# A timetable of slots repacked: latents, routing and the first half of the expert blocks moved to other slots

## The chip, the cores and the metric

The kernel runs on one core of a Trainium2 chip, in float32. Its time is the device time of one execution in microseconds (us). Three executions of the kernel before were timed; one more was taken with the hardware profiler, and all rows shown here come from that one.

The engines are named as the profile names them: PE is TensorE (PEld its weight loads), DVE is VectorE, ACT is ScalarE, POOL is GpSimd, SP is SyncE, which issues most DMAs. Each engine works through its own list of instructions in order. When an instruction waits for a semaphore, everything behind it on the same engine waits too.

## What is computed

Two decoder layers on x of 32 sequences of 128 tokens, width 128. Layer 0: self attention, cross attention over a context, gated experts. Layer 1: causal attention, then an attention of latents over context and latents (2 heads of 64), then 8 ReLU experts of which each token uses two. Only the last two parts matter here, and in outline they are:

```python
# L1 latents: x is both residual and latents; per sequence
ln  = layernorm(layernorm(x))
q, k_l, v_l = split(ln @ [Wq, Wlkv])         # 128 queries, 128 latent keys
k, v = concat(context_kv, (k_l, v_l))        # 256 keys
attn = softmax(mask(rmsnorm(q) @ rmsnorm(k).T))
x = x + (attn @ v) @ Wo + bo
# L1 experts
probs = softmax(layernorm(x) @ router_w + router_b)
topk_w, topk_i = top_k(probs, 2); topk_w /= topk_w.sum()
h = relu(xf @ w1[e] + b1[e]); y = h @ w2[e] + b2[e]
x = x + sum over the token's two experts of gate * y
```

## The kernel before

**Groups and slots.** The 32 sequences ("batches") form 8 groups of 4 (`NG = 4`, `G = 8`). The three attention stages run as one software pipeline over 192 numbered slots, two per batch. Everything else is written into a dictionary `plan` by `at(slot, phase, fn)` and is issued while the loop passes that slot. The phases of a slot come in the order open, pre, (the slot's own score products), inner, (the weighted sums), mid, post. There is no scheduler that reorders: the slot and the phase fix the place in every engine's list. A slot has no fixed length; it lasts as long as the slowest engine needs for what stands in it. After slot 197 no attention is left and a slot holds only what was planned there.

**Stage ends.** `done(2, g)` is the slot after which group g's causal attention is in `X[g]`: 145, 153, ... 201 for groups 0 to 7.

**Latents (`latent_attention`).** Group g starts at `d = done(2, g) + LATER`, with `LATER = 2`. The statistics, normalisation, transposes and the product with `w_lat` take slots d to d + 5. `square`, `total` and `root` give the squared norms of the heads (ACT, DVE, then a power on POOL, L1089); `unit_heads` divides by them at d + 6 or d + 7, phase mid. Then each of the four batches takes four slots, started every second slot from d + 8: `turn` (transposes of q and k, L1136), `score` (L1145, L1150, maxima L1156, exponentials L1157), `turn_e` (L1164, L1166), `weigh` (L1176, L1181). Each of these takes PSUM banks from the pool `ps_m`, which has three. `fetch` loads the batch's context keys and values (`lkv`, 3 buffers) from DRAM two slots ahead of `turn`. `leave` and `project` (L1111, L1118) write the group's result into X at d + 18 and d + 19.

**Routing (`router`).** Groups are routed in units, `UNITS = [(0, 1), (2, 3), (4, 5), (6,), (7,)]`. After the last group of a unit has been projected, the steps `stats`, `scale`, `apply`, `turned`, `choice`, `choose2`, `choose3`, `ranks` follow about one per slot. `ranks` yields for each token and each of its two experts a row of a DRAM array `slots0` (groups 0 to 3) or `slots1` (groups 4 to 7). `scatter` then writes 128 rows with one indirect DMA issued on POOL (L1679), 8 per group, two per slot. A running count per expert, `carry`, passes from unit to unit. `gates_over` and `bias` (L1692, L1705) add the experts' output bias to X.

**Expert blocks (`experts`, `expert_blocks`).** Each half of the tokens is worked off in `NB = 23` blocks of 256 rows. `table` computes from the counts which expert and which rows each block has. `fetch_w` (514 KB, tile `w`, 4 buffers) and `fetch_x` (130 KB, tile `bx`, 10 buffers) are issued on SP, each after a register load from the table. A block takes one slot: `turn(j + 1)` in pre (L1826), `hidden(j)` in inner (L1836, with bias and ReLU shared by ACT and DVE, L1844 and L1846), `result(j - 1)` in post (L1853; scaled by the gates into tile `bo`, 4 buffers, L1861 on ACT and L1863 on DVE), and `leave(j - 2)` in mid: two indirect DMAs on POOL (L1868) that write the rows back to token order. The weights of block j + 3 and the rows of block j + 5 are fetched in post. At slot 203 `swap` closes the pool of the attention tiles and opens the pool `blocks` in the same memory.

```python
            at(done(2, G - 1) + 2, "open", swap)
            begins = [done(2, G // 2 - 1) + 40, done(2, G - 1) + 33]
```

So the first half begins at slot 209 (its first `hidden` stands in slot 211), the second at 234 (first `hidden` in 236). The scatters of the first half's last unit stand in slots 200 to 207, those of the second half's last group in 230 to 233. `gather`, `finish` and `store` add the rows of both experts to X and write the output; for the first half's groups they stand among the second half's blocks, for the second half's they follow the last block.

Of the kernel before, what the change touches and what calls it, by code (L numbers as in the profile page):

```python
# [11 lines left out]
F32 = mybir.dt.float32  # L12
# [10 lines left out]
P = 128  # L23
B, S, D = 32, 128, 128
DC = 96
NG = 4
G = B // NG
# [81 lines left out]
def decoder(ctx: ExitStack, tc: tile.TileContext, a: dict, out: bass.AP):  # L109
# [898 lines left out]
    def latent_attention(lazy, kv, row, bias, masked, plan_route):  # L1008

        LATER = 2  # L1010
        V = []

        def opened():
            if not V:
                for r in range(2):
                    v = lazy["lat"].tile([P, NG, HL, DL + 1], F32, tag=f"v{r}", name=f"lv{r}", bufs=1)
                    nc.gpsimd.memset(v, 1.0)
                    V.append(v)
            return lazy["lat"]

        def plan_group(at, g, d):
            m = {}

# [55 lines left out]
            def flat(u):  # L1079
                return m["qk"][:, 2 * u : 2 * u + 2].rearrange("p b s d -> p (b s d)")  # L1080
# [19 lines left out]
            for u in range(2):  # L1100
                at(d + 4 + u, "mid", square(u))
                at(d + 5 + u, "mid", lambda u=u: m["total", u]())
                at(d + 5 + u, "mid", root(u))
                at(d + 6 + u, "mid", lambda u=u: unit_heads(flat(u), n4, m["nrm", u]))
            for i in range(NG):
                plan_batch(at, m, g, i, d + 8 + 2 * i)

# [13 lines left out]

            at(d + 18, "mid", leave)
            at(d + 19, "mid", project)
            plan_route(at, g, d + 19)

        def plan_batch(at, m, g, i, t):
            b, s = g * NG + i, {}

            def fetch():
                s["kv"] = opened().tile([P, KV], F32, tag="kv", name="lkv", bufs=3)  # L1130
                nc.sync.dma_start(s["kv"][:, P:], kv[b : b + 1].rearrange("b p w -> p (b w)"))
# [36 lines left out]
            def weigh():  # L1168
                if i == 0:
                    m["on"] = opened().tile([P, NG, D], F32, tag="on", name="lon", bufs=1)  # L1170
                vc = s["kv"][:, 2 * P :].rearrange("p (h w) -> p h w", h=HL)
                av = bank(ps_m)[:, : HL * (DL + 1)].rearrange("p (h w) -> p h w", h=HL)
                for h in range(HL):
                    for c in range(2):
                        v = m["v"][:, i, h, :] if c == 0 else vc[:, h, :]
                        nc.tensor.matmul(  # L1176
                            av[:, h, :], s["eT"][:, 2 * h + c, :], v,
                            start=(h == 0 and c == 0), stop=(c == 1), skip_group_check=True,
                        )
                rz = small.tile([P, HL], F32, tag="lrz", name="lrz")  # L1180
                nc.vector.reciprocal(rz, av[:, :, DL])  # L1181
                nc.vector.tensor_tensor(
                    m["on"][:, i, :].rearrange("p (h d) -> p h d", d=DL), av[:, :, :DL], wide(rz, [P, HL, DL], 2), ALU.mult
                )
# [7 lines left out]
        def beside(at, done):  # L1192
            for g in range(G):
                plan_group(at, g, done(2, g) + LATER)
        return beside
# [329 lines left out]
    N2 = 2 * NG  # L1525
    UNITS = [(0, 1), (2, 3), (4, 5), (6,), (7,)]
    HALVES = [(0, 1), (2, 3, 4)]

    def router(slots, lazy):
# [8 lines left out]
        def plan_route(at, g, t):  # L1538
# [198 lines left out]
            def turned(u):  # L1737
# [3 lines left out]
                return fn  # L1741

            for u in us:
                at(t + 1 - 8 * (us[-1] - u), "mid", stats(u, 0))
                at(t + 2 - 8 * (us[-1] - u), "pre", stats(u, 2))
            at(t + 2, "mid", scale)
            for u in us:
                at(t + 3 + u, "mid", apply(u, 0))
                at(t + 4 + u, "pre", apply(u, 2))
                at(t + 4 + u, "mid", turned(u))  # L1750
            t += us[-1]
            at(t + 5, "mid", choice)
            at(t + 6, "mid", choose2)
            if len(groups) > 1:
                t += 1
            at(t + 6, "mid", choose3)
            at(t + 7, "mid", ranks)
            n = 0
            for k in range(n2):
                for c in range(2):  # L1760
                    at(t + 8 + n // 2, ("pre", "inner")[n % 2], scatter(c, k))
                    n += 1
            for u in us:
                at(t + 8 + u, "mid", gates_over(u))
                at(t + 9 + u, "mid", bias(u))

        return plan_route, [carry[units[-1]] for units in HALVES]

    def expert_blocks(f, total, lazy):
# [5 lines left out]
        def table():  # L1775

            def row(shape, tag, dtype=F32):
                return lazy["blocks"].tile([1] + shape, dtype, tag="tb_" + tag, name="tb_" + tag, bufs=2 if tag == "where" else 1)

# [68 lines left out]
        def result(j):  # L1848
            s = state[j]
            ps = bank(ps_t)  # L1850
            for u in range(2):
                for c in range(4):
# [3 lines left out]
                    )  # L1856
            o = s["o"] = lazy["blocks"].tile([P, 2, D], F32, tag="o", name="bo", bufs=4)
            for u in range(2):
# [31 lines left out]
    def experts(halves, lazy, heads, late):  # L1890

        def beside(at, done):
# [3 lines left out]

            at(done(2, G - 1) + 2, "open", swap)
            begins = [done(2, G // 2 - 1) + 40, done(2, G - 1) + 33]

            def plan_half(f):  # L1900
# [3 lines left out]
                for j in range(3):  # L1904
                    at(t - 3 + j, "post", lambda j=j: fetch_w(j))
                for j in range(5):
# [217 lines left out]
```

## Time and profile before

| what | value |
|---|---|
| timed executions | 1186.5, 1189.68, 1194.54 us; median 1189.68 |
| the profiled execution's own time | 1213.03 us |
| its span, first to last instruction | 1211.2 us |
| mean granted TensorE clock | 0.951 |
| PE busy | 1107.3 us, 91% of the span |
| DVE busy | 808.4 us, 67% |
| POOL busy | 632.4 us, 52% |
| ACT busy | 572.9 us, 47% |
| last score product of the attention (L584) starts | 885.2 us |
| first block's `hidden` (L1836) starts | 949.95 us |
| second half's first `hidden` starts | 1097.25 us |
| last product of the blocks (L1853 group) ends | 1185.5 us |

How to read it: the profiled execution lies 23.4 us above the median of the timed ones, so a row of the profile is not by itself a piece of the time that is measured. A busy PE is not a PE at full speed: the column PEclk of the stretches gives the share of the clock that was granted in each. The clock came in two values here, 1.0 and 0.5.

### The profile page before, as it was taken

The numbers are of one execution on the slowest core, as the hardware profiler recorded it, in microseconds if no ns is written. First come the engines' busy times: TensorE is split into PE (matmuls) and PEld (weight loads), VectorE is DVE, ScalarE is ACT, GpSimd is POOL, SyncE is SP. The second block draws the span as 40 slices with busy tenths as digits, with TensorE's granted clock in tenths as the row PEclk, the third lists the DMA queues.
The fourth block names the chain that finished last, engine by engine and source line by source line (L and its number), as shares of the span: only waits on it lengthen the run. The fifth ranks groups of instructions, "written<-read, shape, count | busy, mean of one in ns | idle before, by whom it ended". The sixth has DMA issues, their size and how long they took to land. (4 is left out here: it accounts for less than half of the span.)

```text
span 1211.2 us, 30676 instructions
## 1 busy us (share of the span) xinstructions
PE 1107.3 (91%) x11923; PEld 818.1 (68%) x11923; DVE 808.4 (67%) x2290; ACT 572.9 (47%) x1302; POOL 632.4 (52%) x905
## 2 busy tenths in 40 slices
PE   8999999999999999999999999989988898888991
PEld 3576776676666676656666666666666688777991
DVE  4688888777877877677667678768666564353441
ACT  2355556666655555554445655644553432322330
POOL 3654555344345335434637664746747356664663
PEclk8899999999999999999999999989987898898996
DMA  7705333101021100111020000000102244445873
GB/s 201 240 22 178 99 99 99 54 28 37 3 45 45 46 21 18 37 37 37 2 50 2 11 15 14 15 10 28 32 19 98 93 141 129 145 142 161 256 227 107
DMA packets 83081, 92.09 MB, mean 76 GB/s; under 512 B 14274, under 2 KB 70264, under 8 KB 82928
## 3 DMA queue, kind: packets, MB, share of 16 engines
q1 hardware_dynamic: 77936, 81.57, 23.1%
q0 software_dynamic: 4992, 8.48, 2.0%
q8 instruction: 96, 1.57, 0.5%
q14 instruction: 57, 0.47, 0.1%
HBM read 53.84 MB, written 38.01 MB: 76 GB/s over the span
## 5 line engine op out<-in xcount | busy, mean ns | idle before, releaser
L595 ACT ACTIVATE e<-bank 128x512 f32<-128x512 f32 x384 | 208.1, 595 | 221.6 <-PE bank L584 213.6
L587 DVE TENSOR_REDUCE msc<-bank 128x4 f32<-128x512 f32 x384 | 245.8, 681 | 68.5 <-PE bank L584 67.0
L584 PE MATMUL bank<-kb,qz 32*128 32x256 f32 x1536 | 237.5, 412 | 7.8 <-DVE msc L587 6.1
L584 PE MATMUL bank<-qa,kb 32*128 32x128 f32 x3072 | 233.4, 288 | 1.6 <-ACT e L595 1.6
L584 PEld LDWEIGHTS bank<-qa,kb 32*128 32x128 f32 x3072 | 194.7, 190 | 4.5 <-ACT e L595 3.5
L584 PEld LDWEIGHTS bank<-kb,qz 32*128 32x128 f32 x1536 | 141.9, 189 | 78.8 <-issue 42.2
L1868 POOL DMA_INDIRECT y<-bo,bx x92 | 91.7, 997 | 87.7 <-ACT bo L1861 65.8
L612 PE MATMUL bank<-e,vt 128*32 128x128 f32 x3072 | 126.5, 282 | 2.4 <-POOL e L598 2.4
L598 POOL TENSOR_SCALAR_AFFINE_SELECT e<-e 128x512 f32<-128x512 f32 x128 | 79.1, 642 | 94.4 <-ACT e L595 94.2
L1853 PE MATMUL bank<-w,bh 128*128 128x128 f32 x736 | 95.4, 285 | 1.0 <-issue 0.9
L1853 PEld LDWEIGHTS bank<-w,bh 128*128 128x128 f32 x736 | 92.7, 201 | 4.8 <-issue 3.3
L1836 PE MATMUL bank<-bxT,w 128*128 128x256 f32 x368 | 93.0, 396 | 2.7 <-DVE bh L1846 1.0
L612 PEld LDWEIGHTS bank<-e,vt 128*32 128x32 f32 x3072 | 73.0, 110 | 27.8 <-POOL e L598 3.9
L1679 POOL DMA_INDIRECT slots<-rows,r_ati x64 | 63.8, 997 | 32.6 <-issue 16.5
L1836 PEld LDWEIGHTS bank<-bxT,w 128*128 128x128 f32 x368 | 69.9, 201 | 13.2 <-issue 2.0
L891 POOL TENSOR_TENSOR h<-h,g 128x512 f32<-128x512 f32 x30 | 37.6, 1271 | 71.5 <-DVE nm_st L798 44.8
L1846 DVE TENSOR_SCALAR bh<-bank,w 128x256 f32<-128x256 f32 x92 | 40.2, 478 | 43.9 <-PE bank L1836 35.1
L1861 ACT ACTIVATE bo<-bank,bx 128x128 f32<-128x128 f32 x46 | 16.9, 367 | 96.8 <-PE bank L1853 56.5
L323 ACT ACTIVATE xn<-x,ln_nb,ln_rs 128x128 f32<-128x128 f32 x96 | 42.1, 494 | 41.0 <-POOL ln_nb L317 41.0
L493 DVE SCALAR_TENSOR_TENSOR qa<-bank,head_rows,qz 128x128 f32<-128x128 f32 x192 | 57.6, 342 | 2.2 <-PE bank L485 2.2
L1844 ACT ACTIVATE bh<-bank,w 128x256 f32<-128x256 f32 x92 | 38.6, 471 | 40.1 <-PE bank L1836 15.1
L1157 ACT ACTIVATE le<-bank,lmx 128x256 f32<-128x256 f32 x64 | 26.9, 471 | 64.1 <-DVE lmx L1156 56.7
(322 smaller groups left out, 2280.9 us busy)
## 6 DMA issues: line engine op xcount, KB each, us to landing
w<-in_w_f SPq DMA_DIRECT2D x46, 514.0 KB
slots<-nowhere SPq DMA_DIRECT2D x8, 2340.0 KB
g<-spread SPq DMA_DIRECT2D x16, 512.0 KB
bx<-slots SPq DMA_DIRECT2D x46, 130.0 KB
kv<-kcv SPq DMA_DIRECT2D x8, 516.0 KB
lkv<-kv SPq DMA_DIRECT2D x32, 129.0 KB
y<-y SPq DMA_DIRECT2D x16, 256.0 KB
x<-in_x SPq DMA_DIRECT2D x8, 256.0 KB
```

Source lines behind the costliest of these rows:

```text
L323: nc.scalar.activation(m["xn"][:, i, :], X[g][:, i, :], AF.Identity, scale=m["rs"][:, i : i + 1], bias=m["nb"][:, i : i + 1])
L493: nc.vector.scalar_tensor_tensor(s["qa"][:, u, :], s["mp"][:, :P], head_rows[:, 1 - u : 2 - u], m["qz"][:, u, i * P : (i + 1) * P], ALU.mu ...
L584: nc.tensor.matmul(o, l, r, start=start, stop=stop, skip_group_check=True)
L587: nc.vector.tensor_reduce(tops(MSC[bb % 4], 2 * h + j), sc[j].rearrange("p (s n k) -> p s n k", s=2, n=2), AX.X, ALU.max, negate=True)
L595: nc.scalar.activation(e.rearrange("p n q -> p (n q)"), tr[j], AF.Exp, scale=SCALE)
L598: nc.gpsimd.affine_select(out=e, in_=e, compare_op=ALU.is_ge, fill=0.0, base=0, pattern=[[0, 4], [1, P]], channel_multiplier=-1)
L612: nc.tensor.matmul(s3["av"][32 * n : 32 * n + 32, h3 * P : (h3 + 1) * P], m3["vt"][:, i3, h3, n, u, :], es[u][:, n, :], start=(h3 == 0 and ...
L1679: ins = nc.gpsimd.indirect_dma_start(slots[f], bass.IndirectOffsetOnAxis(ap=m["ati"][:, c, n : n + 1], axis=0), m["rows"][c][:, n, :], Non ...
L1836: nc.tensor.matmul(ps[:, c * BLOCK : (c + 1) * BLOCK], s["w"][:, (2 * k + c) * P : (2 * k + c + 1) * P], s["xT"], start=True, stop=True,)
L1846: nc.vector.tensor_scalar(s["h"][:, n, :], p, bias, 0.0, ALU.add, ALU.max)
L1853: nc.tensor.matmul(ps[:, u * P : (u + 1) * P], s["h"][:, c, u * P : (u + 1) * P], s["w"][:, 512 + c * P : 512 + (c + 1) * P], start=(c == ...
L1868: ins = nc.gpsimd.indirect_dma_start(y, bass.IndirectOffsetOnAxis(ap=s["x"][:, u, D : D + 1].bitcast(U32), axis=0), s["o"][:, u, :], None, ...
```

## The change

In slots, before and after:

| | before | after |
|---|---|---|
| latents of group g start | done + 2 | done + 2, group 7: done |
| first batch's `turn` | d + 8 | d + 6 |
| batches per slot | one every second slot | group 7: one per slot |
| `unit_heads` | mid | pre of the same slot |
| units of routing | (4, 5) together | (4,) and (5,) |
| steps of routing | about one per slot | two per slot, in mid and the next pre |
| scatters of unit (2, 3) | 200 to 207 | 195 to 202 |
| scatters of group 7 | 230 to 233 | 220 to 223 |
| swap of the pools | 203 | 202 |
| first half: table, weights, rows, first `hidden` | 205, 206 to 208, 209, 211 | 199, all three at 202, 203, 205 |
| second half: the same | 230, 231 to 233, 234, 236 | 222, 223 to 225, 226, 228 |
| last `hidden` of the first half | 233 | 227 |

The buffers of `lkv` go from 3 to 6, of the latents' `lon` from 1 to 2, of `bo` from 4 to 6. The small tiles of `table` move to the pool `route`, since the table is now made before the pool `blocks` exists. Gather, finish and store of the first half keep their distance from the second half's begin.

```diff
@@ latent_attention
+        steps = [2] * (G - 1) + [1]
...
-            m = {}
+            m, step = {}, steps[g]
...
-                at(d + 6 + u, "mid", lambda u=u: unit_heads(flat(u), n4, m["nrm", u]))
+                at(d + 6 + u, "pre", lambda u=u: unit_heads(flat(u), n4, m["nrm", u]))
             for i in range(NG):
-                plan_batch(at, m, g, i, d + 8 + 2 * i)
+                plan_batch(at, m, g, i, d + 6 + step * i)
...
-            at(d + 18, "mid", leave)
-            at(d + 19, "mid", project)
-            plan_route(at, g, d + 19)
+            end = d + 6 + step * (NG - 1) + 4
+            at(end, "mid", leave)
+            at(end + 1, "mid", project)
+            plan_route(at, g, end + 1)
...
-                s["kv"] = opened().tile([P, KV], F32, tag="kv", name="lkv", bufs=3)
+                s["kv"] = opened().tile([P, KV], F32, tag="kv", name="lkv", bufs=6)
...
-                    m["on"] = opened().tile([P, NG, D], F32, tag="on", name="lon", bufs=1)
+                    m["on"] = opened().tile([P, NG, D], F32, tag="on", name="lon", bufs=2)
...
-                plan_group(at, g, done(2, g) + LATER)
+                plan_group(at, g, done(2, g) + (LATER if steps[g] > 1 else 0))
@@ router
-    UNITS = [(0, 1), (2, 3), (4, 5), (6,), (7,)]
-    HALVES = [(0, 1), (2, 3, 4)]
+    UNITS = [(0, 1), (2, 3), (4,), (5,), (6,), (7,)]
+    HALVES = [(0, 1), (2, 3, 4, 5)]
...
+            steps = []
             for u in us:
-                at(t + 1 - 8 * (us[-1] - u), "mid", stats(u, 0))
-                at(t + 2 - 8 * (us[-1] - u), "pre", stats(u, 2))
-            at(t + 2, "mid", scale)
+                ago = 8 * (us[-1] - u)
+                at(t - ago, "post", stats(u, 0))
+                at(t + 1 - ago, "pre", stats(u, 2))
+            steps.append(scale)
             for u in us:
-                at(t + 3 + u, "mid", apply(u, 0))
-                at(t + 4 + u, "pre", apply(u, 2))
-                at(t + 4 + u, "mid", turned(u))
-            t += us[-1]
-            at(t + 5, "mid", choice)
-            at(t + 6, "mid", choose2)
-            if len(groups) > 1:
-                t += 1
-            at(t + 6, "mid", choose3)
-            at(t + 7, "mid", ranks)
+                steps += [apply(u, 0), apply(u, 2)]
+            steps += [turned(u) for u in us]
+            steps += [choice, choose2, choose3, ranks]
+            for n, fn in enumerate(steps):
+                at(t + 1 + (n + 1) // 2, ("mid", "pre")[n % 2], fn)
+            t += 1 + (len(steps) + 1) // 2
...
-                    at(t + 8 + n // 2, ("pre", "inner")[n % 2], scatter(c, k))
+                    at(t + n // 2, ("pre", "inner")[n % 2], scatter(c, k))
...
-                at(t + 8 + u, "mid", gates_over(u))
-                at(t + 9 + u, "mid", bias(u))
+                at(t + u, "mid", gates_over(u))
+                at(t + 1 + u, "mid", bias(u))
@@ expert_blocks
-                return lazy["blocks"].tile([1] + shape, dtype, tag="tb_" + tag, name="tb_" + tag, bufs=2 if tag == "where" else 1)
+                return lazy["route"].tile([1] + shape, dtype, tag="tb_" + tag, name="tb_" + tag, bufs=2 if tag == "where" else 1)
...
-            o = s["o"] = lazy["blocks"].tile([P, 2, D], F32, tag="o", name="bo", bufs=4)
+            o = s["o"] = lazy["blocks"].tile([P, 2, D], F32, tag="o", name="bo", bufs=6)
@@ experts
-            at(done(2, G - 1) + 2, "open", swap)
-            begins = [done(2, G // 2 - 1) + 40, done(2, G - 1) + 33]
+            at(done(2, G - 1) + 1, "open", swap)
+            begins = [done(2, G - 1) + 2, done(2, G - 1) + 2 + NB]
...
-                    at(t - 3 + j, "post", lambda j=j: fetch_w(j))
+                    at(t - 3 + j if f else t - 1, "post", lambda j=j: fetch_w(j))
```

## The prediction

> **What bounds the kernel now.** I read the page first. PE is busy 91% of the span, so the question is which of its time is not work. The changed slots lie behind the last score product (885.2 us) and before the last block, so I asked for stretches of that part:
>
> ```profile
> core 0: us, PE busy (x) PEld busy (x) DVE busy (x) ACT busy (x) POOL busy (x), PEclk, DMA share, GB/s
> 918.00:950.00 32.00, 24.55 (x115) 16.78 (x114) 20.59 (x68) 14.67 (x39) 24.52 (x33) 0.72 0.41 130
> 950.00:1012.00 62.00, 60.11 (x420) 53.96 (x420) 33.11 (x109) 21.39 (x55) 26.89 (x33) 0.95 0.36 117
> 1012.00:1042.00 30.00, 24.63 (x124) 21.49 (x124) 13.02 (x54) 5.18 (x13) 19.86 (x24) 0.77 0.37 120
> 1042.00:1075.00 33.00, 31.95 (x221) 28.56 (x220) 18.87 (x74) 11.02 (x28) 21.03 (x26) 1.00 0.52 170
> 1075.00:1104.00 29.00, 20.10 (x108) 16.58 (x108) 6.88 (x18) 5.56 (x14) 14.61 (x15) 0.82 0.42 128
> 1104.00:1184.00 80.00, 80.00 (x563) 75.67 (x562) 35.51 (x89) 25.57 (x64) 47.83 (x46) 1.00 0.70 219
> ```
>
> The last row is the yardstick: blocks alone, PE full, clock 1.00, a block every 3.73 us (`hidden` at 1105.65 and 1109.39). Three rows fall short of it, in busy time and in clock: 918 to 950 (latents alone, before the first block), 1012 to 1042 (inside the first half), 1075 to 1104 (between the halves).
>
> To size the loss I price PE's list at the spacing of starts that the same lines show at full clock: 0.111 us for a float32 pass of 128 columns, 0.216 for 256, 0.324 for 384. So priced, PE's list holds 39.2 us of work from the last score product to the first `hidden`, 113.8 from there to the second half's first, 79.8 after it. The trace took 64.7, 147.3 and 88.3. Lost: **25.5, 33.5 and 8.5 us**.
>
> The timelines of PE, ACT and SP, and the waits of 885 to 1104, tell what the second loss is:
>
> ```profile
> 1016.40 0.31 PE L1653 MATMUL bank<-r_both,ones 128*128 128x32 f32 x2 [1.07 <-issue]
> 1018.02 0.37 ACT L1861 ACTIVATE bo<-bank,bx 128x128 f32<-128x128 f32 x1 [8.33 <-remote]
> ```
> ```profile
> ACT bo L1861 <- remote: 22.5, 4, 8.3
> ```
> ```profile
> 1086.27 3.73 PE L1853 MATMUL bank<-w,bh 128*128 128x128 f32 x32
> 1095.26 0.66 PE L1826 MATMUL bank<-ident,bx 128*128 128x128 f32 x2 [5.25 <-DMA bx<-slots]
> ```
>
> Four times ACT stands still, 22.5 us in all, for a releaser the profile can't name, while PE waits between two products that depend on nothing new ("issue") and SP takes 0.7 us for a register step that elsewhere takes 0.03. The profiled execution is 23.4 us above the median: I take these stops as belonging to it, not to a timed run. Without them 67.5 - 22.5 = **45 us are lost**, 25.5 of them before the first block.
>
> **The change, part by part.**
>
> *Work moved.* The changed PE list, priced the same way, holds 27.8, 116.5 and 81.7 us: 226.0 against 232.8, so 6.8 us (a batch's latents and routing of groups 2 to 4) now stand among the last score products. PE is nearly full there, so I count them as moved, not saved. Before the first `hidden` stand 11.4 us less: group 7's `w_lat` product 2.6, some three batches' steps 7.4, and others. They now stand beside blocks.
>
> *The first hole.* Before, PE reached 27.8 us of this work at about 926 us, 13 us lost; the other 11.4 us took it until 950, 12.5 lost. Those 12.5 are what the earlier blocks can fill. At one place a rule stands against so much: the Trainium skill, TensorE: Matmul & The Clock Gate, section "HAM oscillation — how this bites in real kernels", puts the slow clock down to idle gaps of over some 3.4 us. The longest here is 2.45 us, so by the rule only the idle 32.0 - 24.55 = 7.5 us of 918 to 950 can be had. By the row the granted clock is 0.72, half from 918.4 to 928.7 where no gap is over 1.1 us: many short gaps do it too, and 16.7 us are lost (32 less 15.3 of priced work). I take the row.
>
> *Does the first block have its rows?* PE is in order, so `turn(0)` in slot 204 blocks everything if `bx` isn't there, latents too. The rows come from POOL:
>
> ```profile
> 904.79 1.12 POOL L1679 DMA_INDIRECT slots<-rows,r_ati  x1 [6.12 <-DVE rows L1674]
> 912.43 1.68 POOL L1089 TENSOR_TENSOR nrml<-nrml,half 128x8 f32<-128x8 f32 x1 [5.24 <-DVE nrml L947]
> 938.77 0.97 POOL L1679 DMA_INDIRECT slots<-rows,r_ati  x1 [0.30 <-issue]
> ```
> ```profile
> 941.07 3.65 SPq L1818 DMA_DIRECT2D bx<-slots  x5
> ```
>
> Sixteen scatters took 35 us, and the first `bx` went out 1.3 us after the last. After the change POOL's list between the first and last of them holds 19 scatters at 1.28 (three are already group 4's) 24.3, mask selections 2.5, the scales of group 6's latents and group 4's routing 5.4, two powers 3.4, the rest 2.5: 38 us. `ranks` of unit (2, 3) stands in slot 194, some 15 us earlier by the trace, so the first scatter is due at about 890, the last at 928 with no waits, at 933 with a wait like the 5.24 above. Issue 1.3, transfer 1.4 (1093.83 to 1095.26): rows at 931 to 936. PE itself arrives at 892 + 27.8 + 13 = 933. I take a wait of 2 us; ends 0 and 5. The weights, three at slot 202 (3.1 us from issue to landing each), lie in that cover. First `hidden` at about 935, lost 15 instead of 25.5: **-10.5 us**. SP behind this wait holds two `lkv` loads, needed two slots later; six buffers let the earlier ones go sooner.
>
> *Denser latents beside blocks.* Group 7's batches share each mid: up to five banks of three. A bank waits for DVE's maximum (0.38) and ACT's exponential (0.42); in 950 to 1012 such waits were 0.4 to 1.4 us a batch. With four batches closer I add **1.5 us** (0 if block work covers them, 6 at 1.5 a batch).
>
> *Half a slot instead of one* between POOL's power and `unit_heads`, and between `scale` and `apply`: DVE or ACT blocks if POOL is late, with the ReLUs of the next block behind it. At 874.11 the power ends 1.67 later, when DVE has just finished the attention's 'pre' work: 0.2 us. Taken at 0; up to 1 us for each of 10 late places. On the other side the inserted work may fill gaps among the score products: -3. I keep 0.
>
> *The unit (4, 5) split:* some 33 DVE operations at 0.19 and 2 us on POOL more, in a stretch where DVE is busy 13 of 30 us: 0; 2 if not covered.
>
> *Between the halves.* `where`, weights and rows of the second half stand eight slots sooner, its last scatters three slots before the fetch instead of one. But the weights cross: its first two `w` are asked for before the first half's last, so with four buffers the third waits on SP for `result(21)`, and all `bx` stand behind it. Then SP needs 0.3 for the weights and 0.9 for the register and `bx`, the transfer 1.4 to 2.5: PE idles some 3.5 us at `turn(0)`. Before, without the stop, the rows came about 1.8 us after `result(22)`. **+2 us**; ends -3 (the clock stays up) and +6 (rows behind 514 KB of weights, clock halved). The first half's last weights have 3.7 us where they need 3.5: 0, +1.
>
> *Buffers of `bo`* from 4 to 6: 0 if the stops are the profiler's. The end after the last block (1185.5 to 1211.2) stays.
>
> Sum: -10.5 + 1.5 + 2 = **-7 us**. Against the profiled time 1213.0 this gives 1206; the median of the timed runs lies 23.4 lower: **1182.5 us**, 0.6% faster. A measurement of this kernel can tell about 1% (11.9 us) from no change.
>
> **Rivals.**
>
> *The stops are real (faster).* For: they begin when POOL issues indirect DMAs back to back (1000 to 1016, 1019 to 1034, 1068 to 1081), as four per slot at 1.28 need 5.1 us; ACT stands at `bo`, whose buffers POOL frees; six would give it two slots more, and 24 scatters stand beside the first half's blocks instead of 32. Against: SP and PE stand too, which hold no `bo`; POOL's `leave` at 1006.48 went out right behind ACT's `bo`, so it was not behind; and the 23.4 us. If two thirds of 22.5 go on top: 1182.5 - 15 = 1167.5.
>
> *POOL becomes the bound (slower).* From the first scatter to the first half's last `leave` its list holds 38 + 75 x 1.28 + 17 = 151 us; PE needs 140.4 priced plus what it loses, some 25. In slots 217 to 223 it holds 16 scatters and 14 writes, 40 us, where PE has 26.5. It decides once its in-order waits pass some 15 us; in the trace it waited 11.4 us for DVE in the first chain alone. At 35 us of waits the first rows come 10 us late and half the clock goes after it, and the last scatters hold the second half's first rows: +20 us, 1202.5. Against: by slot 216 POOL has caught up, since it waits for PE's blocks.
>
> *It doesn't do what it says:* the first block stands in slot 205 in the changed lists; it can only be late, which is the rival before.
>
> **How the numbers follow.** Forecast, small gain: 0.48, of which 0.38 within 1% and 0.10 faster (ends of the terms: -18 to +6, so 1172 to 1196). Stops real: 0.30, of which 0.28 faster, 0.02 within. POOL bound: 0.22, 0.17 slower by over 1% and 0.05 within. Sums: faster 0.38, same 0.45, slower 0.17. The range takes all but the tails of both rivals: 1163 to 1201.
>
> **What would show it.** First `hidden` at 933 to 938; the granted clock before it above 0.72; PE idle 3 to 5 us at the second half's first transposes, released by `bx`; POOL back to back from slot 217. ACT's wait at `bo` for "remote" near 20 us again speaks for the forecast, near 5 with a median under 1175 for the first rival. Idle PE of over 6 us at the first block's transposes speaks for the second. A first `hidden` at 935 with no gain at all would prove the sum wrong.

## The result: 3.5% slower, and the profile after

The changed kernel takes 1231.82 us (median of four executions, 1229.59 to 1233.58) against 1189.49 us for the kernel before on the same chip: ratio **1.035, 95% interval 1.031 to 1.039**. The forecast was 1182.5 us, and the range given ended at 1201. The profiled execution has an own time of 1229.59 us and a span of 1227.8 us; unlike that of the kernel before it agrees with its timed runs. Lines of the code move down by two or three: `turn` of the blocks is L1828, `hidden` L1838, `result` L1855, POOL's power L1091, `turn_e` L1169, `lon` L1185.

First the stretches that the prediction spoke of, cut at the events themselves: from 650 us to the last score product, on to the first `hidden`, on to the second half's first, on to the last block.

```profile
core 0: us, PE busy (x) PEld busy (x) DVE busy (x) ACT busy (x) POOL busy (x), PEclk, DMA share, GB/s
650.00:917.60 267.60, 240.11 (x2602) 169.47 (x2604) 175.89 (x509) 132.39 (x321) 148.62 (x219) 0.91 0.06 16
917.60:975.00 57.40, 44.32 (x242) 33.16 (x239) 32.09 (x122) 18.22 (x47) 35.25 (x50) 0.67 0.23 71
975.00:1112.70 137.70, 125.04 (x851) 110.88 (x850) 77.80 (x272) 47.12 (x121) 81.55 (x97) 0.96 0.45 141
1112.70:1197.00 84.30, 84.30 (x571) 79.25 (x571) 36.44 (x91) 26.19 (x65) 47.72 (x46) 0.97 0.68 218
```

The first row is the news. The prediction put no loss there beyond 6.8 us of moved work; the last score product comes at 917.6 us instead of 885.2, with a clock of 0.91. The same row of the kernel before:

```profile
650.00:885.20 235.20, 220.98 (x2604) 154.93 (x2602) 175.79 (x479) 133.90 (x326) 147.04 (x219) 0.97 0.06 17
```

Counted from the same score product (number 3,600 of 4,608, at 655.8 us before and 650.2 after), the changed kernel loses 38.0 us up to the last one. Of that 6.9 us are the moved work; PE is idle 27.5 us in its row instead of 14.2, which makes 13.3; the granted clock is half for 47.8 us instead of 13.7, and half of the difference is an estimate of what that costs, 17. Sum 37.2.

The second stretch is 57.4 us, with a clock of 0.67, for 27.8 us of priced work: 29.6 lost where the forecast had 15. PE is idle for 13.1 of them (57.40 less 44.32); the rest goes with the clock, which is half for 37.5 us of the stretch. The third takes 137.7. The kernel before took 147.3, but 22.5 of that were its stops, so it is 13 us longer than without them, 2.7 of it moved work.

### How a short wait of DVE holds PE

One group's slots among the score products show it. In the kernel before, the power (POOL) and DVE's list around it:

```profile
739.97 1.64 POOL L1089 TENSOR_TENSOR nrml<-nrml,half 128x8 f32<-128x8 f32 x1 [1.99 <-DVE nrml L947]
```
```profile
739.80 1.28 DVE L587 TENSOR_REDUCE msc<-bank 128x4 f32<-128x512 f32 x2
741.00 0.16 DVE L1181 RECIPROCAL lrz<-bank 128x2 f32<-128x2 f32 x1
741.19 0.29 DVE L1182 TENSOR_TENSOR lon<-bank,lrz 128x128 f32<-128x128 f32 x1
...
742.43 0.38 DVE L953 TENSOR_SCALAR nrml<-nrml 128x8 f32<-128x8 f32 x1
```

The power ends at 741.61 us, and DVE comes to `unit_heads` (L953) at 742.43, with the maxima and `lon` already done. The changed kernel, DVE first:

```profile
744.75 0.68 DVE L947 TENSOR_REDUCE nrml<-lsq 128x8 f32<-128x512 f32 x1
747.18 0.59 DVE L953 TENSOR_SCALAR nrml<-nrml 128x8 f32<-128x8 f32 x1 [1.75 <-POOL nrml L1091]
747.80 0.20 DVE L954 RECIPROCAL nrml<-nrml 128x8 f32<-128x8 f32 x1
748.04 0.83 DVE L955 TENSOR_TENSOR lqk<-lqk,nrml 128x512 f32<-128x512 f32 x1
748.80 1.28 DVE L587 TENSOR_REDUCE msc<-bank 128x4 f32<-128x512 f32 x2
749.99 0.16 DVE L1184 RECIPROCAL lrz<-bank 128x2 f32<-128x2 f32 x1
750.18 0.29 DVE L1185 TENSOR_TENSOR lon<-bank,lrz 128x128 f32<-128x128 f32 x1
```

Then POOL, and PE:

```profile
745.51 1.64 POOL L1091 TENSOR_TENSOR nrml<-nrml,half 128x8 f32<-128x8 f32 x1 [1.40 <-DVE nrml L947]
```
```profile
740.96 0.38 PE L584 MATMUL bank<-kb,qz 32*128 32x256 f32 x2
...
747.52 0.70 PE L1153 MATMUL bank<-lkv,lqT 64*128 64x256 f32 x4
750.62 0.41 PE L500 MATMUL bank<-ident,sums 128*128 128x128 f32 x2 [2.40 <-DVE lon L1185]
...
752.65 0.64 PE L584 MATMUL bank<-kb,qz 32*128 32x256 f32 x2
```

`total` (L947) stands on DVE, the power behind it on POOL, and `unit_heads` (L953) half a slot later on DVE again. Nothing stands between them on DVE, so DVE waits 1.75 us for the power. Behind it in order stand `unit_heads` itself, the maxima of the score products (L587) and `lon`, which frees one of the three banks of `ps_m`. PE waits 2.40 us for that bank, and from 752.5 to 756.0 us it has half the clock: a pair of score products that took 0.38 us at 740.96 takes 0.64. A wait of 1.75 us on DVE has cost PE some 4 us, an estimate: the 2.40 and half of the 3.4 at half clock.

The clock does not follow the waits one by one. Of the seven pieces at half clock among the changed kernel's score products, six begin 0.4 to 1.9 us after a gap in PE's work of 1.76 to 2.51 us. The seventh, 20.5 of the 47.8 us, begins at 895.9 us with no gap of over 0.5 us in the 7 us before it, and one gap of 1.76 us (to 880.2) is followed by none. What starts the seventh was not found.

In the kernel before DVE waited for the power once in this stretch. Now it waits eight times:

```profile
DVE nrml L953 <- POOL nrml L1089: 0.6, 1, 0.6
```
```profile
DVE nrml L953 <- POOL nrml L1091: 7.8, 8, 1.8
```

The first line is of the kernel before, the second of the changed one (total, number of waits, longest, in us). PE's waits for `lon` at L500 go with it, in the same order:

```profile
PE bank L500 <- DVE lon L1182: 0.9, 1, 0.9
```
```profile
PE bank L500 <- DVE lon L1185: 7.3, 4, 2.4
```

### The hole before the first block

```profile
943.94 0.18 DVE L1802 CAST tb_where<-tb_first 1x46 int32<-1x46 f32 x1
944.04 0.17 DVE L1630 TENSOR_REDUCE r_w<-r_e 128x4 f32<-128x32 f32 x1
...
947.14 0.19 DVE L1639 TENSOR_TENSOR r_both<-r_picks 128x32 f32<-128x32 f32 x1
947.25 0.16 DVE L1184 RECIPROCAL lrz<-bank 128x2 f32<-128x2 f32 x1
947.45 0.29 DVE L1185 TENSOR_TENSOR lon<-bank,lrz 128x128 f32<-128x128 f32 x1
```
```profile
947.88 2.90 PE L1073 MATMUL bank<-w_lat,lT 128*128 128x384 f32 x4 [4.47 <-DVE lon L1185]
```
```profile
951.92 1.68 POOL L1091 TENSOR_TENSOR nrml<-nrml,half 128x8 f32<-128x8 f32 x1 [11.92 <-DVE nrml L947]
```

`table`, moved to this slot, and then `choose2` and `choose3`, now neighbours, keep DVE for 6.1 us (941.1 to 947.2) ahead of the operation that frees a bank. PE waits 4.47 us. POOL stands 11.92 us at the power with four of the first half's sixteen scatters behind it, and the first `bx` goes out at 967.79 us, 50 us behind the last score product, where the forecast had some 41 (892 to 933). Yet PE does not wait for it: when it reaches `turn(0)` at 973.85 it is later still.

### The profile page after: what moved, and what is told of

Its sections match the earlier page's. It is cut to its first block, busy times and chain, and to the rows that moved or that the text cites. A ratio compares the mean times of both kernels' runs of the same rounds, so it can differ in the third digit from the quotient of the medians.

```text
span 1227.8 us, 30717 instructions
## 1 busy us (share of the span) xinstructions
PE 1115.3 (91%) x11925; PEld 828.6 (67%) x11925; DVE 808.7 (66%) x2323; ACT 573.6 (47%) x1303; POOL 634.7 (52%) x911
## 4 chain that ended last, share of the span: by engine, by line
PE 51%; DVE 17%; POOL 14%; issue 7%; ACT 5%; DMA 4%; SPq 0%; POOLq 0%; DVEq 0%; ACTq 0%
PE bank L584 13%; PE bank L612 5%; DVE msc L587 4%; PE bank L900 3%; POOL y L1870 3%; PE bank L1855 3%; PE bank L1838 2%; PE bank L371 2%; DMA g<-spread 2%; PE bank L882 2%; PE bank L1073 2%; POOL h L891 2%; PE bank L553 1%; POOL nrml L1091 1%; PE bank L485 1%
## 5 line engine op out<-in xcount | busy, mean ns | idle before, releaser
L587 DVE TENSOR_REDUCE msc<-bank 128x4 f32<-128x512 f32 x384 | 245.7, 682 | 73.8 <-PE bank L584 72.7
L584 PE MATMUL bank<-qa,kb 32*128 32x128 f32 x3072 | 237.2, 292 | 1.6 <-ACT e L595 1.6
L584 PEld LDWEIGHTS bank<-qa,kb 32*128 32x128 f32 x3072 | 198.2, 194 | 4.4 <-ACT e L595 2.9
L598 POOL TENSOR_SCALAR_AFFINE_SELECT e<-e 128x512 f32<-128x512 f32 x128 | 80.0, 648 | 116.5 <-ACT e L595 116.3
L1855 PEld LDWEIGHTS bank<-w,bh 128*128 128x128 f32 x736 | 90.9, 197 | 2.5 <-issue 0.3
L1855 PE MATMUL bank<-w,bh 128*128 128x128 f32 x736 | 92.3, 280 | 0.0
L1838 PE MATMUL bank<-bxT,w 128*128 128x256 f32 x368 | 90.4, 390 | 0.0
L1838 PEld LDWEIGHTS bank<-bxT,w 128*128 128x128 f32 x368 | 68.6, 197 | 8.1 <-issue 0.2
L891 POOL TENSOR_TENSOR h<-h,g 128x512 f32<-128x512 f32 x30 | 37.5, 1268 | 70.5 <-DMA g<-spread 34.1
```

What stands on the lines that cost most here:

```text
L584: nc.tensor.matmul(o, l, r, start=start, stop=stop, skip_group_check=True)
L587: nc.vector.tensor_reduce(tops(MSC[bb % 4], 2 * h + j), sc[j].rearrange("p (s n k) -> p s n k", s=2, n=2), AX.X, ALU.max, negate=True)
L598: nc.gpsimd.affine_select(out=e, in_=e, compare_op=ALU.is_ge, fill=0.0, base=0, pattern=[[0, 4], [1, P]], channel_multiplier=-1)
L891: engine.tensor_tensor(m["h"][:, c, :], m["h"][:, c, :], m["g"][:, c, :], ALU.mult)
L1838: nc.tensor.matmul(ps[:, c * BLOCK : (c + 1) * BLOCK], s["w"][:, (2 * k + c) * P : (2 * k + c + 1) * P], s["xT"], start=True, stop=True,)
L1855: nc.tensor.matmul(ps[:, u * P : (u + 1) * P], s["h"][:, c, u * P : (u + 1) * P], s["w"][:, 512 + c * P : 512 + (c + 1) * P], start=(c == ...
```

## The experiments

Absolute times of the kernel before differ by chip: 1189.5 us where the changed kernel was timed, 1196.8 for the first four runs, 1212 to 1218 for the others. So the ratios to the kernel before on the same chip count. The time of a score product inside one profile is sharper: where a kernel has the slots of the kernel before (e6, e7, e10, e11, e13, e14), it agrees with it within about 0.2 us from product 3,600 up to 4,176. Further on it is less sharp: four profiles with the instruction lists of the kernel before on PE, DVE, ACT and POOL (e6, e7, e11, e14) stand at -1.2, 1.2, 4.7 and 4.7 us at the last one, and e4, which has the changed kernel's list that far, at 35.3 instead of 38.0. This table gives the delay against the kernel before, set to zero at product 3,600, before the first group's changed slots (the work moved is priced as in the prediction):

| kernel | at product 3,792 | 3,984 | 4,176 | 4,368 | last | work moved up | ratio, interval |
|---|---|---|---|---|---|---|---|
| changed kernel | 6.3 | 11.5 | 23.3 | 23.1 | 38.0 | 6.9 | 1.035 (1.031 to 1.039) |
| e1 | 6.4 | 14.0 | 27.2 | 32.4 | 55.1 | 6.9 | 1.042 (1.035 to 1.049) |
| e2 | 3.7 | 5.6 | 15.1 | 17.7 | 32.0 | 6.9 | 1.025 (1.018 to 1.032) |
| e3 | 6.3 | 10.8 | 17.4 | 20.3 | 27.2 | 4.4 | 1.027 (1.019 to 1.035) |
| e5 | 3.7 | 4.9 | 7.3 | 15.0 | 22.4 | 4.4 | 1.019 (1.012 to 1.026) |
| e9 | 3.7 | 4.9 | 6.2 | 4.7 | 10.5 | 2.7 | 1.014 (1.010 to 1.019) |
| e8 | 4.7 | 9.1 | 14.8 | 17.6 | 24.9 | 4.4 | 1.024 (1.017 to 1.031) |
| e12 | 4.0 | 8.3 | 13.7 | 18.5 | 25.7 | 0 | 1.022 (1.018 to 1.026) |
| e10 | 0.0 | 0.0 | 0.0 | 1.2 | 3.4 | 1.8 | 1.005 (1.003 to 1.008) |
| e13 | 0.0 | 0.0 | 0.0 | 2.2 | 3.3 | 1.8 | 1.006 (1.004 to 1.009) |

### The half slot: e1, e2, e12, e8

e1, on the changed kernel:

```diff
-                at(d + 6 + u, "pre", lambda u=u: unit_heads(...))
+                at(d + 6 + u, "mid", lambda u=u: unit_heads(...))
```

> unit_heads goes back from the pre phase to the mid phase of its slot; the batches keep their start at d + 6, all else is as in the changed kernel. Theory A (half a slot is too little between POOL's power and unit_heads: DVE waits in order, the maxima of the score products behind it come late, PE loses some 2.4 us per group and half its clock after it): the loss among the score products falls, the last score product starts 12 to 20 us sooner than 917.6 us, the time falls from 1231.8 to 1212-1220 us, and DVE's waits for POOL's power go from 7.8 us (640 to 918 us) to below 2. Theory B (two steps of routing per slot are the loss): no change, 1228-1235 us. Theory C (the earlier expert blocks and scatters are the loss): no change. A doubt for A: the first turn of the batch now stands right behind unit_heads in the same mid, so PE can wait for DVE there; then only half of the gain comes.

1243.48 us, where theory A had it faster: by its ratio slower than the changed kernel (the intervals overlap), and by the table with 55.1 us of delay instead of 38.0. The doubt written down for A is what came. PE's longest total of waits from 650 us to the last score product:

```profile
PE bank L1139 <- DVE lqk L955: 14.1, 6, 3.6
```

The wait for the power, 7.8 us, is gone, but now the first `turn` of the batch (L1139) stands right behind `unit_heads` in PE's list and waits for it directly. With batches from d + 6, pre is too early for the power and mid too late for `turn`.

e2, on the changed kernel:

```diff
-                at(d + 5 + u, "mid", lambda u=u: m["total", u]())
-                at(d + 5 + u, "mid", root(u))
+                at(d + 5 + u, "pre", lambda u=u: m["total", u]())
+                at(d + 5 + u, "pre", root(u))
```

> total and root (the power on POOL) go from the mid phase of slots d + 5 and d + 6 to their pre phase, unit_heads and all else stay as in the changed kernel: the distance between power and unit_heads is a whole slot again. Theory A: 1212-1220 us, as for unit_heads in mid, without its doubt; DVE's waits for the power below 2 us of 640 to 918. Theory B and theory C: no change, 1228-1235 us. If DVE's total now waits for ACT's squares instead, a part of the gain is lost.

1225.47 us, where A had 1212 to 1220. By the ratio, which allows for the other chip, it is 1.0% or about 12 us faster than the changed kernel (the intervals just overlap), the low end of A's 12 to 20. In the table the delay halves, from 11.5 to 5.6 us at product 3,984, and comes back from there on in nearly the same steps as in the changed kernel, where routing stands. DVE's wait for the power falls from 7.8 to 0.6 us; `total` now waits for ACT's squares instead:

```profile
DVE nrml L947 <- ACT lsq L944: 4.3, 5, 0.9
```

So the edit took away most of one short wait and made another. The cleaner trial is the one word put into the kernel before, where no batch moves. e12:

```diff
-                at(d + 6 + u, "mid", lambda u=u: unit_heads(...))
+                at(d + 6 + u, "pre", lambda u=u: unit_heads(...))
```

> The kernel before with one word changed: unit_heads in pre instead of mid of its slot, half a slot behind POOL's power. Theory A (DVE waits in order for the power, the maxima behind it are late, PE waits and the clock halves): about what the opposite edit gave, ratio 1.006 to 1.012, DVE's waits for the power above 6 us, the last score product 8 to 13 us later. If the half slot costs only where the batches follow at d + 6: 0.999 to 1.003.

**1.022**: some 27 us at the 1212.24 us of the kernel before on that chip, about twice the most that theory A had named. No work is moved, and 25.7 us of delay stand at the last score product, 4 to 5 in each of the first four steps. Its stretch, its DVE wait and PE's largest wait in it (650 to 910 us):

```profile
650.00:909.90 259.90, 232.95 (x2585) 161.87 (x2579) 172.65 (x478) 133.10 (x323) 148.48 (x218) 0.92 0.05 15
```
```profile
DVE nrml L953 <- POOL nrml L1089: 11.7, 12, 1.8
```
```profile
PE bank L500 <- DVE lon L1182: 7.7, 4, 2.4
```

The chain of the changed kernel is here alone: 11.7 us of DVE's waits instead of 0.6, 7.7 of PE's at L500 instead of 0.9, and half the clock for 41.0 us instead of 13.7. PE is idle 27.0 us in its row instead of 14.2; these 12.7 and 13.7 for the clock (half of 27.3) are about the 25.7. This edit was expected to show the theory; it shows the size as well.

e8, the kernel before with the whole of the latents' part:

```diff
-                at(d + 6 + u, "mid", lambda u=u: unit_heads(...))
+                at(d + 6 + u, "pre", lambda u=u: unit_heads(...))
-                plan_batch(at, m, g, i, d + 8 + 2 * i)
+                plan_batch(at, m, g, i, d + 6 + 2 * i)
-            at(d + 18, "mid", leave)
-            at(d + 19, "mid", project)
-            plan_route(at, g, d + 19)
+            at(d + 16, "mid", leave)
+            at(d + 17, "mid", project)
+            plan_route(at, g, d + 17)
```

> The kernel before with the latents' part alone: unit_heads in pre, batches from d + 6, leave and project two slots sooner, routing behind them; blocks where they were. If the half slot costs what the changed kernel shows (2 to 2.4 us of wait and half a clock per group), the last score product is 10 to 18 us later than 885 us (some 3 of it work moved up), little of it comes back behind it, and the ratio is 1.006 to 1.014. If the half slot is hidden, 0.997 to 1.003.

1.024, again above the expectation, and no more than e12's one word within the intervals. Two slots sooner for batches and routing add nothing to that which these runs resolve.

### Packed routing: e3 and e10

e3, on the changed kernel: the steps of routing as in the kernel before, and for it

```diff
-            begins = [done(2, G - 1) + 2, done(2, G - 1) + 2 + NB]
+            begins = [done(2, G - 1) + 5, done(2, G - 1) + 5 + NB]
```

> The steps of routing go back to about one per slot, as in the kernel before; scatters and both halves of the blocks come three slots later for it; latents as in the changed kernel. Theory B: PE no longer waits 2.5 us for r_both in front of ranks, nor runs at half clock after it (slots around 798 and 895 us): 10 to 15 us sooner at the last score product, of which the later blocks give back 3 to 5: 1220-1226 us. Theory A: the latents' loss stays, and the later start of the blocks costs some 3 us: 1231-1237 us. Theory C: some 3 us faster per slot that the blocks are later, 1222-1228 us, with the gain behind the last score product.

1224.25 us lies in B's range and not in A's; C had nearly the same range, but with the gain behind the last score product, and that product comes 10 us sooner. So packed routing too costs time in the changed kernel, though by the ratios alone the intervals of the two overlap. The delay between products 3,984 and 4,176, where the first unit is routed, is 6.6 us instead of 11.8; between 4,368 and the last, where the second is, 6.9 instead of 14.9 (2.5 of it work moved back). e10 puts packed routing alone into the kernel before:

```diff
-            at(t + 2, "mid", scale)
...
-            at(t + 7, "mid", ranks)
+            steps += [choice, choose2, choose3, ranks]
+            for n, fn in enumerate(steps):
+                at(t + 1 + (n + 1) // 2, ("mid", "pre")[n % 2], fn)
```

> The kernel before with the routing's part alone: two steps per slot, latents from d + 8 with unit_heads in mid, blocks where they were. If the chain of DVE's small operations (some 28 in a slot and a half) holds PE's banks wherever it stands: the last score product 8 to 14 us later than in the kernel before (some 4 of it work moved up), ratio 1.004 to 1.010. If it costs only together with latents from d + 6: 0.998 to 1.003.

1.0054 lies in the first expectation's range, but not by its mechanism: among the score products the delay is 3.4 us, 1.8 of it moved work. That is within what profiles of one list differ by, so without the latents' half slot packed routing is hidden or nearly hidden there. Behind the last score product e10's profile takes 330.5 us, where the two of the kernel before take 326.0 and 327.6.

### The late part: e4, e7, e11, e14

e4, on the changed kernel:

```diff
-            begins = [done(2, G - 1) + 2, done(2, G - 1) + 2 + NB]
+            begins = [done(2, G - 1) + 8, done(2, G - 1) + 8 + NB]
```

> Only the begins of both halves change: six slots later, 209 and 232, nearly those of the kernel before. Theory C (the earlier blocks collide with scatters and latents): faster than the changed kernel by 8 us or more. Theories A and B: the last score product at 917 us as before the edit, and the time grows by what the earlier start was worth, 5 to 12 us: 1237-1244 us. If the earlier start is worth nothing, 1230-1234 us.

1243.13 us: ratio 1.0416 against 1.035, so theory C falls and the earlier blocks are worth about 8 us to the changed kernel by these two ratios (their intervals overlap). The last score product, at 917.1 us, does not move.

e7 starts from the kernel before and takes the late part alone:

```diff
+        steps = [2] * (G - 1) + [1]
-                plan_batch(at, m, g, i, d + 8 + 2 * i)
+                plan_batch(at, m, g, i, d + 8 + step * i)
-                plan_group(at, g, done(2, g) + LATER)
+                plan_group(at, g, done(2, g) + (LATER if steps[g] > 1 else 0))
-    UNITS = [(0, 1), (2, 3), (4, 5), (6,), (7,)]
+    UNITS = [(0, 1), (2, 3), (4,), (5,), (6,), (7,)]
-            begins = [done(2, G // 2 - 1) + 40, done(2, G - 1) + 33]
+            begins = [done(2, G - 1) + 7, done(2, G - 1) + 7 + NB]
```

(`leave`, `project`, the buffers, `swap`, the table and the fetches follow as in the change.)

> The attention stage's slots as in the kernel before (unit_heads in mid, batches from d + 8, about one step of routing per slot), and the late part as in the changed kernel as far as it goes: group 7 at done with one batch per slot, units (4,) and (5,), more buffers, blocks at 208 and 231 (before 209 and 234). If the two losses among the score products are what made the changed kernel slower, its last score product is at 885 to 890 us and the ratio 0.993 to 1.003. If the denser group 7 and the split unit cost DVE and PE as much behind the attention as the packed routing did, 1.008 to 1.02.

1.0033 (1.0015 to 1.0052): the half slot and the packed routing left out, nearly the whole loss is gone; a gain does not appear, and the ratio ends just above the first expectation. Its stretch from the last score product to the first `hidden` is 70.6 us, where the kernel before takes 64.8, though that `hidden` stands a slot sooner.

e14 is e7 with group 7 at done + 2 again:

```diff
-                plan_group(at, g, done(2, g) + (LATER if steps[g] > 1 else 0))
+                plan_group(at, g, done(2, g) + LATER)
```

> The kernel with the late part only, with group 7's latents at done + 2 as in the kernel before instead of at done; still one batch per slot, units (4,) and (5,), blocks at 208 and 231. The late part alone gave 1.0033. If group 7's start among the last score products is what it loses there (slots 186 to 188, some 3 us, and clock after it): 0.996 to 1.001, the last score product within 1.5 us of the kernel before. If the denser batches behind the attention are the loss: 1.002 to 1.006.

1.0027 (0.9997 to 1.0056). The expectation misplaced the edit: group 7's latents begin at slot 201 or 203, behind the last score product in slot 196, and up to there e7 and e14 issue what the kernel before issues, only with more buffers. So the 1.2 and 4.7 us of delay are not group 7's. Whether the denser batches cost e7 its time, the interval does not tell.

e11, the kernel before with group 7 alone two slots sooner:

```diff
-                plan_group(at, g, done(2, g) + LATER)
+                plan_group(at, g, done(2, g) + (LATER if g < G - 1 else 0))
-            begins = [done(2, G // 2 - 1) + 40, done(2, G - 1) + 33]
+            begins = [done(2, G // 2 - 1) + 40, done(2, G - 1) + 31]
```

The larger `lkv` and `lon` belong to it. Here too only the buffers, and with them three earlier loads of `lkv`, differ from the kernel before up to the last score product; buffers alone were not run.

> The kernel before with group 7's latents two slots sooner (still one batch every second slot) and the second half at 232 instead of 234; nothing among the score products moves. If the gap between the halves is worth what the prediction took for it, some 11 us lost without the stops, two empty slots fewer give 0.994 to 0.998. If PE's work moved out of the gap only waits elsewhere: 0.999 to 1.003.

1.0129 (1.0090 to 1.0167), slower, outside both expectations. All three stretches up to the second half are longer: 4.7 us of delay at the last score product, 74.1 us to the first `hidden`, 157.4 in the first half (64.8 and 147.3 before), with half the clock for 79 us of the last two instead of 49. Why this costs more than e7's denser group is open.

### Together: e5, e9, e13

e5 is e2's and e3's edits at once.

> Both edits at once: total and root half a slot sooner, and the steps of routing about one per slot with scatters and blocks three slots later. The first alone gave a ratio of 1.025 to the kernel before, the second 1.027, the changed kernel 1.035. If they are two separate losses, they add: 1.017 (1.013 to 1.021), the last score product near 900 us. If both shorten the same waits, 1.022 to 1.026. If these two are the whole loss, 1.000.

1.019, in the range of two separate losses that add.

e9 is e5 with `plan_route(at, g, end + 3)` for `end + 1`, and the blocks at 208 and 231.

> As the kernel with both edits (power half a slot sooner, routing about one step per slot, latents from d + 6), but routing starts two slots later, so that it stands in the slots of the kernel before; blocks at 208 and 231. That kernel had a ratio of 1.019 and stretches of 62 us where the kernel before has 54 just where the first unit is routed. If it is routing, two slots sooner, that stands badly among the score products: 1.003 to 1.010, the last score product 10 to 14 us sooner than with routing at once. If the latents themselves cost it from d + 6: 1.016 to 1.021.

The delay at the last score product falls by 11.9 us, from 22.4 to 10.5, inside the expectation for routing that stands badly two slots sooner (1.7 of it is work moved back); the steps between products 4,176 and 4,368, 7.7 us in e5, are gone. The ratio, 1.014, lies between the two expectations, and its interval overlaps e5's. Where the rest of the gain goes is not shown: in the profiles e9 takes no longer behind the last score product than e5 (328.3 and 334.8 us).

e13 is the changed kernel with the latents' part undone:

```diff
-                at(d + 6 + u, "pre", lambda u=u: unit_heads(...))
+                at(d + 6 + u, "mid", lambda u=u: unit_heads(...))
-                plan_batch(at, m, g, i, d + 6 + step * i)
+                plan_batch(at, m, g, i, d + 8 + step * i)
-            end = d + 6 + step * (NG - 1) + 4
+            end = d + 8 + step * (NG - 1) + 4
-            begins = [done(2, G - 1) + 2, done(2, G - 1) + 2 + NB]
+            begins = [done(2, G - 1) + 4, done(2, G - 1) + 4 + NB]
```

> The changed kernel with the latents' part undone: unit_heads in mid, batches from d + 8, and with them routing, scatters and blocks two slots later; packed routing, group 7 (one batch per slot, from done) and the split unit stay. If the parts add, packed routing alone (1.0054) and the late part alone (1.0033) give 1.009 (1.005 to 1.013), the last score product within 6 us of the kernel before. If packed routing and the denser late part cost more together than alone, 1.015 to 1.025, and the half slot is not the main cause of the changed kernel's 1.035.

1.0063 (1.0042 to 1.0085), inside the range for parts that add, and 3.3 us of delay at the last score product. **Of the 3.5% the latents' part makes up 2.9** (2.3 to 3.5 by the ends of the two intervals). Parts alone: 1.024 (e8), 1.005 (e10), 1.003 (e7); their excesses sum to 3.2%, inside the interval of the whole. Both sums compare ratios from different chips, and some of these chips have the stops of the next part; the changed kernel itself was timed only on one whose profile has none. What packed routing does behind the score products shows in e13's waits of PE from 883 to 1110 us:

```profile
PE bank L1654 <- DVE r_both L1639: 9.2, 3, 6.0
PE bank L1654 <- DVE lon L1185: 7.2, 1, 7.2
```

The product of `ranks` waits for DVE's chain of small operations, which now stands half a slot ahead of it; in e6, the kernel before, PE waits for `r_both` there once, 0.5 us.

### The stops: e6

> The kernel before, profiled a second time. If the four stops of ACT at bo for a releaser without a name (22.5 us) belonged to the one execution, as the prediction has it: none of them, an own time of 1185 to 1200 us, and 123 to 127 us instead of 147.3 from the first half's first hidden to the second half's. If they are the kernel's: again some 20 us of them.

Own time 1212.06 us, and 149.1 us from the first half's first `hidden` to the second's. The stops are there again:

```profile
ACT bo L1861 <- remote: 13.6, 2, 8.3
```

The timed runs of the kernel before on that chip have a median of 1215.79 us. So the stops do not belong to one execution, as the prediction had it, but come back on some chips, in timed runs too by their medians; the profiles of e1 to e4 and of the changed kernel, on others, name none. During the stops the other engines stand still or creep while POOL issues indirect DMAs one after the other, 0.97 us each with 0.30 between. What causes it was not found. No version here beats the kernel before.

## Why the prediction was wrong, point by point

**The step that failed: "Half a slot instead of one … Taken at 0; up to 1 us for each of 10 late places."** It was sized at one place, 874.11 us, where the attention's own operations keep DVE busy until 0.2 us before the power ends. At 745 us nothing stands between, and DVE waits 1.75. Measured alone (e12) the term is 25.7 us among the score products, where the sum had 0 and its bound 10. The mean wait is 1 us (11.7 over 12), so on the mean the bound of 1 us for a place even held for DVE. What was left out is what stands behind: the maxima, the bank and PE, which is idle 12.7 us longer, and then the clock, some 13.7 more.

**Two steps of routing per slot** were not priced as a step at all, beyond that half slot. Alone they cost 0.5% (e10); beside the latents' half slot they cost more: with the steps spread again the changed kernel loses 10.8 us less up to its last score product (e3), 2.5 of it work moved back.

**The first hole, −10.5 us: wrong.** First `hidden` at 975.0 us, 57.4 behind the last score product where 43 was forecast (892 to 935), and the clock before it was 0.67, not above 0.72. The rows were late, sent 50 us behind the last score product instead of some 41, for the reason that the rival "POOL becomes the bound" named, an in-order wait of POOL (11.92 us at one power). But PE, held by DVE and at half clock, came later still, so the rival's price was not paid either. Its time (1202.5) had the right sign and the wrong engine.

**Between the halves, PE idle some 3.5 us at `turn(0)`: right.**

```profile
1111.01 0.66 PE L1828 MATMUL bank<-ident,bx 128*128 128x128 f32 x2 [4.37 <-DMA bx<-slots]
```

**Denser latents and the split unit: not separated.** The third stretch loses 21.2 us (137.7 less 116.5 of priced work). Before it lost 11.0 without the stops, and the sum added 3.5 for the denser latents and the second half's start. The other 6.7 us are not explained.

**The work moved, 6.8 us: right,** but it came among score products that did not take it for free.

**The stops: subtracted rightly, explained wrongly.** The chip that timed both kernels has a median of 1189.49 us, so by their time the stops were not in those runs; by these profiles they belong to other chips, not to an execution (e6). The rival "the stops are real" could gain nothing on that chip: compared without them, the changed kernel's profile is 39 us slower. Nor do six buffers of `bo` end them: on e6's chip e7, which has six, shows stops at `bh` instead (11.3 us in two waits).

**The clock: the row was right against the rule.** The Trainium skill (TensorE: Matmul & The Clock Gate, "HAM oscillation — how this bites in real kernels") puts the slow clock down to gaps of over some 3.4 us. In e12 PE's list of waits up to the last score product names none over 2.6 us, and it has 41.0 us at half clock, against 13.7. But the prediction drew that conclusion for the hole it wanted to fill, and not for the short waits that the change itself would make.

## What to carry to other kernels

Where engines work through fixed lists, price a new wait by everything behind it: the next instructions on that engine, the buffer they free, the engine that needs the buffer, and that engine's clock; here one microsecond of DVE's waiting cost PE two (11.7 and 25.7 us, e12). The handover from DVE to POOL and back was hidden with a slot between its ends and not with half a slot, though POOL works on it for only 1.64 us, and it was shortened where PE was 94% busy. Before a schedule is repacked, try each distance that shrinks by itself in the old kernel: the one word of e12 would have told most of it.

## What the hardware showed unexpectedly

The slots are reproducible far better than whole runs: slots with the same list mostly take the same time within some 0.2 us, on different chips too (now and then one differs by 1 to 2 us), so a delay of a few microseconds can be placed in one profile. PE's clock goes to half for 3.4 us or a multiple of it, often within 2 us of a wait as short as 2.40 us (ended at 750.62; half clock from 752.5): in e12 eight of the nine such pieces up to the last score product begin within 2.5 us of the end of a gap in PE's work of 1.1 to 2.5 us, yet the changed kernel's longest does not. And the same kernel takes 1189 us on one chip, 1197 on another and 1212 to 1218 on three more; on one of these, a profile has two stops of ACT for an unnamed releaser, 13.6 us in all, while POOL issues indirect DMAs.
